# A decoder layer on one core: 512 KB transfers cut into quarters, other buffers for the end's temporaries, new dates for the planner

## The chip, the cores and the metric

The kernel runs on one core of one Trainium2 chip. The core has four engines that compute: PE (TensorE, matrix products), DVE (VectorE), ACT (ScalarE) and POOL (GpSimd). SP (SyncE) issues nearly all DMAs here. The metric is the device time of one execution in microseconds (us); lower is better.

## The reference

One decoder layer over 8 batches of 512 rows and 256 columns, in float32, each of its three parts followed by a layer norm:

```python
# gated linear attention in chunks of 32 rows, with decay
S = jnp.einsum('bncd,bnkd->bnck', Qc, Kc) * mask
O = jnp.einsum('bnck,bnkd->bncd', S, Vc).reshape(B, T, D)
x1 = ln(x + (sigmoid(x @ W_g.T) * O @ W_o.T + x))
# cross attention, 16 heads of 64, over a context of 512 rows
a = softmax(where(key_mask, q @ k.T / 8, -inf))
x2 = ln(x1 + ((a @ v) @ Wo + bo))
# FFN, 1024 wide: ternary weights, a low-rank term, squared relu
h = bitlinear(x2, w_fc) + gate * (x2 @ v.T @ fast_b.T @ u.T)
out = ln(x2 + bitlinear(relu(h)**2, w_proj))
```

## The kernel before

The kernel keeps float32 accuracy by splitting each operand into two float16 halves, high and low, and adding three products of halves (`PASSES`, line 43). A split is two instructions: one engine casts the high half, another subtracts it from the source.

**Units.** The bulk is the cross attention. `units` holds one entry for each batch b, pair of heads p (8 of them) and quarter of 128 query rows qt (4): 256 units. Line 451 issues all instructions, so the profile is read by tile names. For one unit, `scores` computes `s` for two heads on PE, DVE adds the mask and takes the extreme (`s`, `nm`), ACT takes the exponential (`e`). `split_p` casts `e` into the high half of `ph`, on ACT or on POOL as `HIGH` says (a or p for qt 0 to 3; the first word is for batch 0, the second for the later ones, the third for pairs 5 to 7 of the last batch), and DVE subtracts for the low half. Two units share one DMA transpose of `ph` into `pT` (1 MB of float16, issued by SP), and `attend` multiplies it with `v` into `av`. After four units `of` and `oh` scale and split the result, and a DMA transpose makes `oT` of it. The last two pairs of the last batch go through smaller pieces, `ofl` and `ohl`, and through PE instead of a DMA.

**Other work between the units.** Generators hold it: `gen_l0` (linear attention of the next batch; it loads `xs` and `row`), `load_ctx` (loads `ctxs` and the mask), `gen_kv`, `gen_q` and `gen_v` (projections), `gen_wo` and `gen_ffn` (output projection and FFN of the batch before), and in batch 0 the preparation of the weights. A `Filler` takes a share of them at each unit; `PULL` is the budget for one unit. `ffn_end` normalizes a finished batch and stores it. The FFN of the last batch has its own form, `ffn_tail`, in two halves of 256 rows, whose steps write `rhl`.

**The planner.** No order is written out by hand. Every instruction is recorded with a date (`nc.prio`): the unit's number plus an offset of `LATE` for its kind of work. `Recorder.cost` gives it a duration, and `Recorder.schedule` plays the engines through: whenever an engine is free it gets the ready instruction with the earliest date whose tiles have a free buffer. `REACH` bounds how far past the first candidate it looks. The order found so is emitted, one queue for each engine. SP's queue holds loads, stores and transposes in one line. The dates are thus numbers that change the order on all engines and not the instructions.

**The end.** After the last unit the fixed numbers `TP` date the rest: `bf.drain` (what remains of batch 6's FFN), the last `attend`s, `wo_tail`, the two halves of `ffn_tail`, and batch 6's `ffn_end`.

**Buffers.** A tag is a ring of buffers that a tile waits for. The change touches `t4` (5), `tmp2` (4), `pT` (3), `ph` (3), `x1T` (2) and `ctxh` (2).

Of the kernel before, what the change touches and what calls it, by code (L numbers as in the profile page):

```python
# [11 lines left out]
F16 = mybir.dt.float16  # L12
# [14 lines left out]
LAG = 4  # L27
BURST = 2
MARGIN = 0.0
REACH = 9.52  # L30
SPARE = 1
DLATE = 1.6
PTS = 3
PHS = 3
NWP = 4
TP = (0.35, 0.96, 1.15, 3.0, 0.5, 5.1)
STICK = 2.09
HOLD = 0.18
HIGH = ("apaa", "paaa", "papp")
LATE = {"k": 0.0, "q": 0.0, "v": 0.53, "w": -0.33, "l": -0.41, "o": -0.91, "f": 0.31, "s": 0.0, "a": 0.91, "t": 0.0, "x": 0.31, "e": 0.0, "c": -1.28, "d": -0.95}  # L40
PULL = {"k": 5.13, "l": 2.62, "w": 3.61, "f": 4.71, "g": 5.48}

PASSES = ((0, 0), (0, 1), (1, 0))

# [109 lines left out]
class Recorder:  # L154
# [96 lines left out]
    def cost(self, o, ins, outs):  # L251

        n = max([int(np.prod(x.shape[1:])) for x in outs + ins] or [0]) if o.engine != "PE" else outs[0].idx.size
        psum = any(x.t.pool[:2] == "ps" for x in ins + outs)
        ones = sum(x.idx.size == 1 and x.t.free > 0 for x in ins)
        o.half, o.port = None, o.engine == "POOL"
        o.dma = o.method[:3] == "dma"
        if o.dma:
            x = (outs or ins)[0]
            if o.method == "dma_start_transpose":  # L260
                blocks = n / 128
                o.occ, o.lat = 0.1 * blocks + 0.4, 0.115 * blocks + 0.55
            else:
                size = {F32: 4, F16: 2}.get(x.t.dt, 1)
                o.occ, o.lat = 0.45, n * size * x.shape[0] / (380e3 if self.prio < 0 else 210e3) + (1.2 if size == 1 else 0.1)
        elif o.engine == "PE":
            o.occ = n / 2400 + 0.0025
            o.lat = o.occ + 0.17
            if ins[0].p1 - ins[0].p0 == 64:
                o.half = ins[0].p0  # L270
        elif o.engine == "DVE":
            lat = 0.145 + n * 1.042e-3
            if o.method == "tensor_tensor_reduce":
                o.occ, o.lat = 0.615, 0.8
                return
            if not psum and o.method in ("tensor_copy", "tensor_scalar") and n >= 512:
                lat = 0.12 + n * 0.62e-3
            if psum and ones and o.method == "scalar_tensor_tensor":
                lat += 0.065
            if n <= 8:  # L280
                lat = 0.19 if o.method == "reciprocal" else 0.175 if o.method == "bn_aggr" else 0.145
            o.occ, o.lat = lat - 0.085, lat
            o.port = not psum and o.method in ("tensor_tensor", "scalar_tensor_tensor", "tensor_scalar", "tensor_copy")
        elif o.engine == "ACT":
            lat = 0.165 + n * 0.83e-3 + (0.0 if psum else 0.04) + 0.07 * ones
            o.occ, o.lat = (lat + 0.01, lat + 0.12) if "accum_out" in o.kw else (lat - 0.11, lat)
        elif o.engine == "POOL":
            if o.method == "tensor_tensor":
                lat = 0.3 + n * 1.67e-3 if n <= 512 else 0.2 + n * 1.9e-3
                if o.args[3] == ALU.pow:  # L290
                    lat = 0.42 + 0.16 * n
            else:
                lat = 0.13 + n * 0.9e-3 if n > 512 else 0.92 if n == 256 and o.kw == {} and o.method == "tensor_scalar" and o.args[-1] == ALU.is_lt else 0.62 if n > 256 else 0.56 if n > 8 else 0.22 + n * 5e-3
            o.occ, o.lat = lat - 0.03, lat
# [178 lines left out]
def decoder_kernel(ctx: ExitStack, tc: tile.TileContext, ins: dict, out: bass.AP):  # L473
# [270 lines left out]
    def split_in(src, b, nm, ring):  # L744
        stg = wk.tile([128, 2, 2, T], F32, tag="pT", name=f"{nm}s{b}", bufs=PTS)[:, 0] if ring and b == 1 else t4(f"{nm}s{b}", [128, 2, T], F32)
        sv = src[:, b * T:(b + 1) * T].rearrange("(c p) n -> p c n", p=128)
        if ring and b != 1:
            xh = t4(f"{nm}h{b}", [128, 2, 2, T])
        else:
            xh = wk.tile([128, 2, 2, T], F16, tag="ctxh", name=f"{nm}h{b}", bufs=2)  # L750
        if b == 0:
            for c in range(2):
                nc.sync.dma_start(stg[:, c], sv[:, c])
        else:
            nc.sync.dma_start(stg, sv)

        def cast():
            if b == 0:
                for c in range(2):
                    nc.scalar.copy(xh[:, 0, c], stg[:, c])  # L760
                    nc.vector.tensor_tensor(xh[:, 1, c], stg[:, c], xh[:, 0, c], ALU.subtract)
            else:
                for c in range(2):
                    nc.gpsimd.tensor_scalar(xh[:, 0, c], stg[:, c], 1.0, 1.0, ALU.mult, ALU.mult)
                    nc.gpsimd.tensor_tensor(xh[:, 1, c], stg[:, c], xh[:, 0, c], ALU.subtract)
        return xh, cast
# [60 lines left out]
    def gen_l0(b):  # L827
# [32 lines left out]
            nc.vector.tensor_tensor(v0[:, 1, 2 * tt:2 * tt + 2, :], pv, v0[:, 0, 2 * tt:2 * tt + 2, :], ALU.subtract)  # L860
            yield 6
        if b:
            nc.sync.dma_start(row, ins["x"][b].rearrange("(t p) n -> p t n", p=128))
        th = t4(f"th{b}", [128, 2, T], F32)
        for m in range(2):
            ps = misc(f"pg{b}{m}")
# [158 lines left out]

    def ffn_end(b):
        layernorm(b, rows[b], EPS, "c")
        nc.sync.dma_start(out[b].rearrange("(t p) n -> p t n", p=128), rows[b])

    def ffn_tail(b, i, base, step_):  # L1030
        row = rows[b]
        rh, py = {}, {}
        ts = slice(256 * i, 256 * i + 256)
        PL = 3
        for s_ in range(8 + PL):
            nc.prio = base + step_ * s_
            if s_ == 0:
                zst = ffn_z(b, ts, f"{b}_{i}", ("zst", "sph")[i])
            if s_ < 8:
                j = s_  # L1040
                r4 = ffn_h(b, j, ts, zst, f"{b}_{i}", True)
                hl = t4(f"rhl{i}{j}", [128, 2, 256])
                if i == 0 or j % 2:
                    nc.scalar.activation(r4, r4, AF.Square)
                else:
                    nc.vector.tensor_tensor(r4, r4, r4, ALU.mult)
                if j % 2:
                    nc.scalar.copy(hl[:, 0], r4)
                else:
                    nc.vector.tensor_copy(hl[:, 0], r4)  # L1050
                (nc.vector if j % 3 == 2 or (i == 1 and j == 7) else nc.gpsimd).tensor_tensor(hl[:, 1], r4, hl[:, 0], ALU.subtract)
                rh[j] = hl
            if s_ >= PL:
                j = s_ - PL
                if j == 0:
                    for t in range(2):
                        py[t] = misc(f"pyl{i}{t}")[:, :D]
                hl = rh.pop(j)
                for t in range(2):
                    for a in range(2):  # L1060
                        nc.tensor.matmul(py[t], hl[:, a, t * 128:(t + 1) * 128], tpj[:, j, :],
                                         start=(j == 0 and a == 0), stop=(j == 7 and a == 1))
            yield
        for t in range(2):
            tt = 2 * i + t
            y = tmp2(f"yl{tt}", [128, D])
            nc.vector.tensor_tensor(y, py[t], s2b, ALU.mult)
            nc.vector.tensor_tensor(row[:, tt], row[:, tt], y, ALU.add)
            layernorm(b, row, EPS, "c", tt, 1, True)
            nc.sync.dma_start(out[b, tt * 128:(tt + 1) * 128], row[:, tt, :])  # L1070
        yield
# [61 lines left out]
    def attend(u):  # L1133
# [12 lines left out]
        if tail:  # L1146
            if qt == 0:
                oT[b, p] = wk.tile([128, 2, T], F16, tag="oT", name=f"oT{b}_{p}", bufs=8)
            if qt % 2:
                d = den[b, p][:, qt - 1:qt + 1, :]  # L1150
                nc.vector.reciprocal(d, d)
                of = tmp2(f"ofl{p}{qt}", [128, 2, 2, DH])
                nc.vector.scalar_tensor_tensor(of, av[b, p][:, qt - 1:qt + 1], sc, d.unsqueeze(3).broadcast_to([128, 2, 2, DH]), ALU.mult, ALU.mult)
                oh = tmp2(f"ohl{p}{qt}", [128, 2, 2, 128], F16)
                ofv = of.rearrange("p t h n -> p t (h n)")
                nc.scalar.copy(oh[:, 0], ofv)
                nc.vector.tensor_tensor(oh[:, 1], ofv, oh[:, 0], ALU.subtract)
                dst = oT[b, p][:, :, (qt - 1) * 128:(qt + 1) * 128].rearrange("p a (t n) -> p a t n", t=2)
                for a in range(2):
                    pe_T(dst[:, a], [oh[:, a, t_] for t_ in range(2)], f"o{p}{qt}{a}", a)  # L1160
            return
# [85 lines left out]
    def at(i, off):  # L1247
        now[0], nc.prio = i, i + off
# [84 lines left out]
            if pend:  # L1333
                attend(pend.pop(0))

    at(U, 1)
    bf.drain()
    at(U, TP[0])
    rest(len(pend) - 4)
# [63 lines left out]
```

## Time and profile before

| | us |
|---|---|
| median of 3 runs | 1062.81 |
| these runs, lowest and highest | 1061.47, 1063.2 |
| the profiled execution, device time | 1061.94 |
| its span | 1060.1 |
| PE, DVE, ACT and POOL busy in it | 998.2, 986.9, 879.4, 544.8 |
| mean granted clock of PE | 0.988 |

The span runs from the first instruction of the profile to the last; the device time lies 1.84 us above it. A row of busy time by stretches has the stretch, its length, the busy time of each engine with its number of instructions, PE's granted clock, the DMA engines' share and GB/s. In a timeline a row is start, length, engine, operation, tile written and tiles read, and in brackets how long the engine was idle before and what released it. The rows of transfers have KB and the median time from issue to landing. PE's matmuls are pipelined and their ends are modelled, so that a PE at 20.00 of 20 need not be at its peak.

### The profile page before, as it was taken

The page shows a single profiled execution, that of the slowest core. Times are in us where ns is not written, and L with a number is a line of the kernel's source. Part 1 is how long each engine was busy: PE and PEld are TensorE (multiplying, and loading weights), DVE is VectorE, ACT ScalarE, POOL GpSimd, SP SyncE. Part 2 cuts the span into 40 slices and gives each one's busy share as a digit, 9 for nine tenths or more (in the row PEclk, how much of TensorE's full clock was granted, in tenths as well). Part 3 has the DMA queues.
Part 4 walks back from the last instruction along what each step waited for, and adds up shares of the span by engine and source line. Part 5 has one row for each costly group of instructions (what it writes and reads, how often), then busy time and mean ns, then how long its engine had stood idle before and what let it go on. Part 6 is the DMA issues. An engine that isn't in the chain of part 4 may idle for free.

```text
span 1060.1 us, 29949 instructions
## 1 busy us (share of the span) xinstructions
PE 998.2 (94%) x11976; PEld 639.3 (60%) x11976; DVE 986.9 (93%) x2101; ACT 879.4 (83%) x1876; POOL 544.8 (51%) x513
## 2 busy tenths in 40 slices
PE   7986889999999999999999999999999999999986
PEld 4644545665666656665666656766567656665664
DVE  7999989999999989999899989999899998998976
ACT  7787778889977998789977898879977889878836
POOL 0251282256841596245861577426962548443635
PEclk9999989999999999999999999999999999999989
DMA  8289799999999999989999999999999999999861
GB/s 306 99 147 186 133 214 186 164 180 191 186 185 189 174 179 168 207 155 189 185 184 204 162 185 179 192 189 156 195 163 214 154 185 170 187 167 201 138 115 41
DMA packets 646636, 185.65 MB, mean 175 GB/s; under 512 B 628448, under 2 KB 641376, under 8 KB 646496
## 3 DMA queue, kind: packets, MB, share of 16 engines
q1 hardware_dynamic: 645632, 183.42, 95.6%
q8 instruction: 93, 1.52, 0.6%
q10 hardware_dynamic: 864, 0.32, 0.1%
q14 instruction: 47, 0.39, 0.1%
HBM read 21.18 MB, written 4.19 MB: 24 GB/s over the span
## 4 chain that ended last, share of the span: by engine, by line
PE 41%; ACT 17%; DVE 17%; DMA 12%; issue 6%; POOL 4%; SPq 2%; ACTq 0%; POOLq 0%; DVEq 0%
PE av L451 8%; PE s L451 8%; DMA pT<-ph 6%; ACT e L451 6%; DVE s L451 5%; DVE ph L451 5%; PE pk L451 4%; PE pq L451 4%; PE pwo L451 4%; ACT r L451 4%; PE py L451 3%; PE pvv L451 3%; ACT ph L451 3%; SPq L451 2%; DVE W L451 2%
## 5 line engine op out<-in xcount | busy, mean ns | idle before, releaser
L451 ACT ACTIVATE e<-s,nm 128x512 f32<-128x512 f32 x512 | 354.4, 705 | 100.7 <-DVE nm L451 83.3
L451 DVE SCALAR_TENSOR_TENSOR ph<-e,ph 128x1024 f16<-128x1024 f32 x256 | 330.6, 1298 | 27.6 <-ACT ph L451 25.2
L451 DVE CUSTOM_DVE_ANT_0 s<-s,mb 128x512 f32<-128x512 f32 x512 | 342.3, 710 | 6.1 <-PE s L451 4.5
L451 PEld LDWEIGHTS <-pT 128*128 128x128 f16 x6144 | 198.7, 99 | 59.5 <-issue 29.5
L451 PE MATMUL av<-v,pT 128*128 128x64 f16 x6144 | 213.2, 194 | 12.4 <-DMA pT<-ph 12.2
L451 PE MATMUL s<-W 64*128 64x512 f16 x1536 | 205.6, 379 | 12.5 <-ACT e L451 10.8
L451 ACT ACTIVATE ph<-e 128x1024 f16<-128x1024 f32 x186 | 200.0, 1081 | 2.4 <-DMA pT<-ph 0.3
L451 POOL TENSOR_SCALAR ph<-e 128x1024 f16<-128x1024 f32 x70 | 84.8, 1211 | 227.3 <-ACT e L451 214.7
L451 PEld LDWEIGHTS <-W 64*128 64x128 f16 x1536 | 64.2, 94 | 110.4 <-issue 59.4
L451 PEld LDWEIGHTS <-wqkv 128*128 128x128 f16 x768 | 70.3, 98 | 82.6 <-issue 18.0
L451 POOL TENSOR_TENSOR oh<-of,oh 128x512 f16<-128x512 f32 x62 | 86.6, 1396 | 65.0 <-ACT oh L451 63.1
L451 ACT ACTIVATION_READ_ACCUMULATOR e<-s,nm 128x1 f32 x512 | 113.5, 222 | 0.0
L451 PE MATMUL pk<-ctxh,wqkv 128*128 128x512 f16 x384 | 103.0, 382 | 6.2 <-POOL ctxh L451 6.1
L451 PE MATMUL pvv<-wqkv,ctxh 128*128 128x256 f16 x768 | 102.0, 274 | 0.3 <-DVE v L451 0.3
L451 POOL TENSOR_TENSOR rh<-r,rh 128x512 f16<-128x512 f32 x56 | 75.1, 1345 | 52.4 <-ACT rh L451 52.4
L451 PE MATMUL pq<-x1T,wqkv 128*128 128x512 f16 x384 | 97.2, 380 | 0.5 <-DVE bob L451 0.3
L451 PEld LDWEIGHTS <-ctxh 128*128 128x128 f16 x768 | 71.4, 98 | 26.1 <-issue 13.0
L451 PEld LDWEIGHTS <-oT 128*128 128x128 f16 x768 | 73.8, 100 | 20.8 <-issue 5.3
L451 PE MATMUL pwo<-wo,oT 128*128 128x256 f16 x672 | 84.2, 276 | 0.4 <-ACT e L451 0.4
L451 DVE DVE_READ_ACCUMULATOR2_ANT nm<- 128x1 f32 x512 | 72.4, 141 | 0.0
L451 PE MATMUL ph<-x2T,tfc 128*128 128x512 f16 (+1 forms) x288 | 68.4, 356 | 0.3 <-ACT r L451 0.3
L451 PE MATMUL py<-tpj,rh 128*128 128x256 f16 x448 | 58.4, 273 | 0.0
(190 smaller groups left out, 1492.4 us busy)
## 6 DMA issues: line engine op xcount, KB each, us to landing
row<-in_x SPq DMA_DIRECT2D x8, 512.0 KB, 5.4
xs<-in_xT SPq DMA_DIRECT2D x7, 512.0 KB, 4.9
ctxs<-in_ctxT SPq DMA_DIRECT2D x7, 512.0 KB, 4.5
out_dram<-row SPq DMA_DIRECT2D x7, 512.0 KB, 3.6
wqs<-in_wqkv SPq DMA_DIRECT2D x6, 512.0 KB, 7.2
pT<-ph SPq DMA_TRANSPOSE x131, 7.5
wos<-in_wo SPq DMA_DIRECT2D x4, 256.0 KB, 2.8
fcs<-in_w_fc SPq DMA_DIRECT2D x2, 512.0 KB, 4.9
```

The source lines that it names most:

```text
L451: getattr(real[x.engine], x.method)(*[r(a) for a in x.args], **{k: r(a) for k, a in x.kw.items()})
```

## The change

First, transfers: the loads of `xs` and `ctxs` (for batches 1 to 7), those of `row` (batches 1 to 7) and the stores of batches 0 to 6, each 512 KB in one DMA, are issued as four DMAs of 128 KB. Second, buffers at the end: the eight `rhl` tiles of each half of `ffn_tail` become one tile each, in a `pT` and a `ph` buffer; `yl` and `ofl` move from `tmp2` to `x1T`, `ohl` from `tmp2` to `ctxh`. Third, dates: `REACH`, `TP` (which gets a seventh number, for `bf.drain`), `HIGH`, `LATE`, `PULL`, and the planner's duration of a float32 matmul.

```diff
-REACH = 9.52
+REACH = 9.84
...
-TP = (0.35, 0.96, 1.15, 3.0, 0.5, 5.1)
+TP = (0.0, 2.0, 0.8, 3.0, 0.5, 5.1, 2.0)
...
-HIGH = ("apaa", "paaa", "papp")
-LATE = {"k": 0.0, "q": 0.0, "v": 0.53, "w": -0.33, "l": -0.41, "o": -0.91, "f": 0.31, "s": 0.0, "a": 0.91, "t": 0.0, "x": 0.31, "e": 0.0, "c": -1.28, "d": -0.95}
-PULL = {"k": 5.13, "l": 2.62, "w": 3.61, "f": 4.71, "g": 5.48}
+HIGH = ("aapp", "paaa", "appa")
+LATE = {"k": 0.0, "q": 0.0, "v": 0.53, "w": -0.48, "l": -0.41, "o": -0.91, "f": 1.36, "s": 0.0, "a": 0.91, "t": 0.0, "x": 0.31, "e": 0.0, "c": -1.28, "d": -1.57}
+PULL = {"k": 4.04, "l": 2.62, "w": 3.61, "f": 4.71, "g": 4.5}
...
-            o.occ = n / 2400 + 0.0025
+            o.occ = n / 2400 + 0.0025 if ins[0].t.dt is F16 else n / 200
...
-            nc.sync.dma_start(stg, sv)
+            for c in range(2):
+                for h in range(2):
+                    nc.sync.dma_start(stg[:, c, 256 * h:256 * h + 256], sv[:, c, 256 * h:256 * h + 256])
...
-            nc.sync.dma_start(row, ins["x"][b].rearrange("(t p) n -> p t n", p=128))
+            for t in range(4):
+                nc.sync.dma_start(row[:, t], ins["x"][b, t * 128:(t + 1) * 128])
...
-        nc.sync.dma_start(out[b].rearrange("(t p) n -> p t n", p=128), rows[b])
+        for t in range(4):
+            nc.sync.dma_start(out[b, t * 128:(t + 1) * 128], rows[b][:, t])
...
+        rhl = wk.tile([128, 8, 2, 256], F16, tag=("pT", "ph")[i], name=f"rhl{i}", bufs=(PTS, PHS)[i])
...
-                hl = t4(f"rhl{i}{j}", [128, 2, 256])
+                hl = rhl[:, j]
...
-            y = tmp2(f"yl{tt}", [128, D])
+            y = wk.tile([128, D], F32, tag="x1T", name=f"yl{tt}", bufs=2)
...
-                of = tmp2(f"ofl{p}{qt}", [128, 2, 2, DH])
+                of = wk.tile([128, 2, 2, DH], F32, tag="x1T", name=f"ofl{p}{qt}", bufs=2)
...
-                oh = tmp2(f"ohl{p}{qt}", [128, 2, 2, 128], F16)
+                oh = wk.tile([128, 2, 2, 128], F16, tag="ctxh", name=f"ohl{p}{qt}", bufs=2)
...
-    at(U, 1)
+    at(U, TP[6])
     bf.drain()
```

## The prediction

> **What bounds the kernel now.** I read the busy line of the page first, then the chain of work that ended last, then busy time by stretches of 20 us, and last the waits of each engine inside the stretches that have gaps.
>
> ```profile
> PE 998.2 (94%) x11976; PEld 639.3 (60%) x11976; DVE 986.9 (93%) x2101; ACT 879.4 (83%) x1876; POOL 544.8 (51%) x513
> ```
> ```profile
> PE 41%; ACT 17%; DVE 17%; DMA 12%; issue 6%; POOL 4%; SPq 2%; ACTq 0%; POOLq 0%; DVEq 0%
> ```
>
> PE and DVE are busy together, and no engine carries the chain alone. So a time saved on one engine counts only where the other has a gap at the same place. The stretches (PE, PEld, DVE, ACT, POOL busy, clock, DMA) show where that is:
>
> ```profile
> 80.00:100.00 20.00, 14.18 (x184) 8.28 (x181) 19.22 (x50) 17.06 (x37) 4.69 (x5) 1.00 0.94 168
> 240.00:260.00 20.00, 19.58 (x197) 10.56 (x194) 19.88 (x45) 19.88 (x41) 12.23 (x14) 1.00 1.01 192
> 260.00:280.00 20.00, 19.42 (x223) 11.82 (x222) 15.92 (x29) 19.53 (x41) 19.10 (x17) 1.00 1.02 182
> 280.00:300.00 20.00, 20.00 (x260) 13.41 (x257) 20.00 (x48) 16.00 (x35) 13.06 (x13) 1.00 1.04 177
> ...
> 1020.00:1040.00 20.00, 18.00 (x204) 13.94 (x203) 13.93 (x46) 11.74 (x30) 7.41 (x15) 0.91 0.12 23
> 1040.00:1060.00 20.00, 10.97 (x88) 7.54 (x86) 11.99 (x34) 11.50 (x28) 10.93 (x19) 0.88 0.16 53
> ```
>
> Added up over all such rows (20 less PE's busy time), PE idles 21.8 us in 40 to 160 (batch 0, where the weights are still prepared), 16.2 us in all of 160 to 960, and 16.4 us from 960 on. The middle repeats every 122 to 124 us, and its one weak place per batch is the row 260 to 280: ACT full, DVE at 15.9. The timeline of DVE there says why:
>
> ```profile
> 267.13 1.32 DVE L451 SCALAR_TENSOR_TENSOR ph<-e,ph 128x1024 f16<-128x1024 f32 x1 [3.60 <-ACT ph L451]
> ```
>
> DVE waits 3.60 us for ACT's half of a split (`ph`), because ACT is working off `r`, its square and its cast for the FFN of the batch before. The same wait (3.54 to 3.60) comes back at 389, 513, 635, 757 and 881.
>
> **The change part by part.**
>
> *Quarters.* 7 loads of `xs`, 7 of `ctxs`, 7 of `row` (batch 0's stays) and 7 stores become 112 transfers, 84 issues more.
>
> ```profile
> out_dram<-row SPq DMA_DIRECT2D x7, 512.0 KB, 3.6
> ...
> out_dram<-row SPq DMA_DIRECT2D x4, 128.0 KB, 1.7
> ```
> ```profile
> 305.43 0.52 SPq L451 DMA_DIRECT2D out_dram<-row  x1
> 306.36 5.64 SPq L451 DMA_TRANSPOSE pT<-ph  x1
> ```
>
> An issue holds SP's queue for 0.52 us, so 84 cost it 44 us. The queue's transposes hold it 131 x 4.94 + 62 x 1.3 + 14 x 3 = 770 us of 1060, so there is room on the average; but a `pT` transpose issued right behind a group comes 3 x 0.52 = 1.6 us later than now. Queued behind are only transposes, and PE's `av` waits for those:
>
> ```profile
> PE av L451 <- DMA pT<-ph: 12.2, 10, 2.4
> ```
>
> The gain is bounded by those of the 10 waits that stand beside a transfer that is cut: 1.64 us at 139.75 (loads at 136.3 and 136.9) and 1.21 at 921.5 (a store at 918.1), 2.9 together; the others, 2.42 and 2.28 at 963 and 1015 above all, have only transposes before them. The loss, if every delay were bare, is 28 x 1.6 = 45 us. Both ends are far from the usual case: 10 waits on 131 `pT` transposes mean that nearly every one of them has slack, so I stay near nothing: -0.5.
>
> [...] The two rows above (3.6 and 1.7) agree that a quarter costs far more than a quarter, but nobody waits for these loads in the middle, and no run yet shows four of them issued behind one another.
>
> *Dates of the middle* (`LATE["f"]` 0.31 to 1.36, `PULL["k"]` 5.13 to 4.04, `LATE["d"]`, `REACH`). No instruction is added or removed. The FFN's work of the batch before loses priority against split and softmax by a whole unit, which is the wait of 3.60 us above; what is late next is PE, idle in the six ACT-bound rows by 0.58 + 0.78 + 1.07 + 1.21 + 1.61 + 1.21 = 6.5 us. If the six DVE waits (21.5 us) went altogether, PE's 16.2 us of gaps would be the limit. Below nothing: the FFN's pieces put off must be done before their batch ends, in rows where DVE or PE stands at 20.00, and the 9.7 us of PE gaps outside the six rows are as good a size for a loss as for a gain. Nearest to the row of the six gaps, less than half of it: -2.5.
>
> *Batch 0* (`HIGH[0]` from apaa to aapp, `LATE["w"]`, the planner's cost of an f32 matmul). Eight splits go from ACT (1.065 us each, 8.5 in all) to POOL (1.047, 8.4). PE waits 7.0 us for ACT's `e` between 60 and 160, the bound of the gain. The price is on DVE, which is at 20.00 from 20 to 80 and at 19.22 in the next row: its `ph` takes 1.19 us alone and 2.02 beside POOL work:
>
> ```profile
> 999.86 1.19 DVE L451 SCALAR_TENSOR_TENSOR ph<-e,ph 128x1024 f16<-128x1024 f32 x1
> ...
> 1004.73 2.02 DVE L451 SCALAR_TENSOR_TENSOR ph<-e,ph 128x1024 f16<-128x1024 f32 x1
> ```
>
> So 0 to 8 x 0.83 = 6.6 us more, and POOL's 29.2 us of waiting for ACT's `e` there say that it has the time itself. Two f32 matmuls (`ps`, 1.21 us, after a wait of 2.15 for `dg`) are now known to the planner as long, worth about 1 us. Halves of both bounds cancel (-3.5 and +3.3); I take -1 with that one.
>
> [...]
>
> *The end* (`HIGH[2]` from papp to appa, `TP`, buffers, `PULL["g"]`). From 983 to 1008 the chain is DVE. Three more splits leave POOL: 3 x 0.83 = 2.5 us at most off DVE, while ACT idles 2.01 and 2.52 us before its `e` at 1001.8 and 1007.6 and so can take 1.065 each; I take -1.5. The drain of batch 6 put off by one unit takes `y` (0.67, in the chain at 1004.13) out of the way: -0.5. From 1032 to 1052 ACT is the limit (17.06 of 20 busy). The waits for `rhl` there (1.12, 0.42, 0.49 on ACT) are for the ring of three that holds `r4`, which stays; no wait names the ring of five that `rhl` leaves. So the new buffers free the order rather than remove a wait: between 0 and 2.9 us (20 less 17.06); with the earlier start of the first half's steps (0.8 apart for 1.15) I take -1. Below nothing: three splits that delay ACT's `e` by 1.065 each, +3.2. Together -3, between -6 and +3.
>
> **Sum.** -0.5 - 2.5 - 1 - 3 = -7.0 against the profiled execution: span 1060.1, device time 1061.94, so 1054.9. The median of the three runs, 1062.81, lies 0.87 above that execution; added, 1055.8.
>
> **Rivals.**
> (1) *SP's queue becomes the wait.* Quarters are issued in a row ahead of transposes that have no slack. PE's weight loads for `av` already wait in 23 places and PE in 10, so a third of the 28 groups is thinkable: 28 x 1.6 / 3 = 15 us, less the 6.5 of the other parts, 1062.8 + 8.5 = 1071. It decides from where 6.5 of the 45 us is bare, that is from one group in seven (4 of 28). For it: DMA shares of 1.0 to 1.2 in the middle. Against: 290 us free in the queue.
> (2) *The new dates only move the gaps.* PE and DVE are at 20.00 in the rows after 280, and the work that fills the gap is missed there; only a microsecond or two of the end remains: 1061.5.
> (3) *The ACT-bound row dissolves.* All of PE's 16.2 us in the middle go, and the end gives 3: 1062.8 - 19.2 = 1043.6. For it: ACT has 4 us free in the row behind. Against: in 280 to 300 DVE and PE are both full already.
>
> **How the numbers follow.** The forecast gets 0.54, rival 1 0.20, rival 2 0.14, rival 3 0.12. Less than 0.2% (2.1 us) can't be told from no change, so faster is 0.54 + 0.12 = 0.66, same 0.14, slower 0.20. The forecast's own range is 1055.8 with -7 and +5: half of the bounds of the middle and the end. The asked range reaches to rival 1 at 1071 and, below, to 1046, which leaves out half of rival 3 and the larger half of rival 1's bad cases.
>
> **What would show it.** Quarters: PE's wait for `pT` stays near 12 us, and SP shows groups of four issues or ones parted by transposes; a wait above 20 means rival 1. Middle: the six DVE waits of 3.6 us are gone or shorter, the period of a batch falls by about 0.4 us from 122 to 124; if the period stands, rival 2. Batch 0: POOL's `ph` count is 75 for 70, DVE's mean `ph` there rises from 1.29 us. End: from the last `e` to the last store less than the 50 us of now, DVE's `ph` near 1004 at 1.2. The prediction is wrong if the period grows, or if DVE's extra time in batch 0 is paid in full.

## The result, and the profile after

| | before | after |
|---|---|---|
| median (lowest to highest, runs), us | 1062.92 (1061.47 to 1063.2, 4) | 1076.02 (1072.72 to 1078.71, 4) |
| ratio, 95% interval | | 1.0125 (1.0109 to 1.0141) |
| profiled execution, span, us | 1061.94, 1060.1 | 1075.25, 1073.5 |
| mean granted clock of PE | 0.988 | 0.980 |

The changed kernel is 1.25% slower, 13.1 us by the medians; 1055.8 had been forecast, within 1046 to 1071. The page after, its busy line and its chain of work that ended last:

```profile
PE 1002.4 (93%) x11976; PEld 639.3 (60%) x11976; DVE 995.0 (93%) x2101; ACT 879.6 (82%) x1871; POOL 552.8 (51%) x518
...
PE 42%; DVE 26%; DMA 10%; ACT 9%; issue 7%; POOL 6%; SPq 0%; ACTq 0%; DVEq 0%; POOLq 0%
```

PE runs the same 11,976 matmuls in 4.2 us more, DVE the same 2101 instructions in 8.1 us more. ACT's part of the chain fell from 17% to 9% and DVE's rose from 17% to 26%: ACT, which the forecast saw as the weak place of the middle, holds less of the chain, and the time is longer.

**Where the time went.** DVE adds the mask to each unit's scores (`s`), so the start of that instruction dates a unit. Differences of these dates (units 0 to 31 are batch 0, 224 to 255 the last batch) give the stages, in us; each row adds up to its span:

| from, to | before | after | difference |
|---|---|---|---|
| start, unit 0 | 45.4 | 45.1 | -0.3 |
| 0, 16 | 57.3 | 69.6 | +12.3 |
| 16, 32 | 65.4 | 63.7 | -1.7 |
| 32, 224 | 730.2 | 742.1 | +11.9 |
| 224, 255 | 109.7 | 105.3 | -4.4 |
| 255, last instruction | 52.1 | 47.6 | -4.5 |

So batch 0 lost 10.6, the six middle batches 11.9, and the end won 8.9. The stretches of after (PE, PEld, DVE, ACT, POOL busy, granted clock, DMA share, GB/s):

```profile
80.00:100.00 20.00, 13.27 (x172) 7.82 (x168) 15.78 (x39) 11.64 (x26) 6.97 (x7) 0.74 0.95 173
...
270.30:290.30 20.00, 16.58 (x179) 8.71 (x176) 17.01 (x28) 19.51 (x41) 19.87 (x16) 1.00 1.14 192
290.30:310.30 20.00, 19.87 (x259) 13.75 (x256) 20.00 (x43) 15.84 (x33) 13.53 (x12) 1.00 1.09 189
```

Batch 0: from 80 to 100 DVE went from 19.22 busy to 15.78 and the clock from 1.00 to 0.74. Middle: unit 32 comes 10.3 us later in after, so its rows are set 10.3 us later than those of before from 260 on. There DVE rose only from 15.92 to 17.01, while PE fell from 19.42 to 16.58 and ACT stayed full (19.53 and 19.51); the next rows are nearly alike. The ends are compared by their distance from the last instruction, since after's comes 13.4 us later. The two stretches from 60 to 20 us ahead of it, of before and then of after:

```profile
1000.10:1020.10 20.00, 17.03 (x267) 13.47 (x263) 16.86 (x33) 8.13 (x22) 9.56 (x7) 0.91 1.18 189
1020.10:1040.10 20.00, 18.00 (x204) 14.02 (x203) 13.93 (x46) 11.84 (x30) 7.51 (x15) 0.91 0.11 22
```
```profile
1013.50:1033.50 20.00, 19.01 (x289) 13.88 (x288) 18.55 (x38) 17.06 (x38) 10.36 (x8) 1.00 1.21 199
1033.50:1053.50 20.00, 19.64 (x241) 16.23 (x240) 15.96 (x47) 11.59 (x30) 10.81 (x18) 1.00 0.22 51
```

PE idles 5.0 us of these 40 before and 1.4 after, and DVE 9.2 and 5.5: the end is denser.

**Batch 0.** PE's timeline of after (start, length, what, and in brackets the idle time before it), then the same place of before:

```profile
79.51 1.57 PE L451 MATMUL av<-v,pT 128*128 128x64 f16 x48
86.03 2.74 PE L451 MATMUL av<-v,pT 128*128 128x64 f16 x48 [4.95 <-DMA pT<-ph]
88.71 1.88 PE L451 MATMUL s<-W 64*128 64x512 f16 x7
```
```profile
78.07 0.82 PE L451 MATMUL s<-W 64*128 64x512 f16 x6
...
80.51 0.82 PE L451 MATMUL s<-W 64*128 64x512 f16 x6
83.12 1.57 PE L451 MATMUL av<-v,pT 128*128 128x64 f16 x48 [1.80 <-DMA pT<-ph]
```

In before, scores of later units go ahead of the `av` that waits for a transpose; the wait is 1.80 us, and DVE has scores to work on. In after, the next scores (unit 10's) stand behind that `av`: PE is idle for 4.95 us, DVE starts no scores between 74 and 90.3, and both pieces then run at a granted clock of 0.51 (the mean from 84.9 to 95.1), the `av` in 2.74 us for 1.57. The order of SP's queue changed as well. Its timeline, of before and then of after:

```profile
73.51 2.53 SPq L451 DMA_TRANSPOSE tfc<-fct  x2
76.21 4.89 SPq L451 DMA_TRANSPOSE pT<-ph  x1
```
```profile
70.01 2.50 SPq L451 DMA_TRANSPOSE tfc<-fct  x2
72.61 9.82 SPq L451 DMA_TRANSPOSE pT<-ph  x2
```

In before the third `pT` goes ahead of two transposes of the FFN's weights (`tfc`), in after behind them, and it waits for the low half of the sixth `ph`, which ends at 71.1 for 67.8, since DVE did other work first. The fourth `pT`, for which the `av` at 86.03 waits, then follows with no gap: it starts 1.3 us later than in before, and the `av` behind it 2.9 us later.

### The profile page after: what moved, and what is told of

It reads as the page before. It is cut to its first block, busy times and chain, and to the rows that moved or that the text cites. A ratio compares the mean times of both kernels' runs of the same rounds, so it can differ in the third digit from the quotient of the medians.

```text
span 1073.5 us, 30062 instructions
## 1 busy us (share of the span) xinstructions
PE 1002.4 (93%) x11976; PEld 639.3 (60%) x11976; DVE 995.0 (93%) x2101; ACT 879.6 (82%) x1871; POOL 552.8 (51%) x518
## 4 chain that ended last, share of the span: by engine, by line
PE 42%; DVE 26%; DMA 10%; ACT 9%; issue 7%; POOL 6%; SPq 0%; ACTq 0%; DVEq 0%; POOLq 0%
PE s L451 8%; DVE s L451 8%; PE av L451 8%; DMA pT<-ph 8%; DVE ph L451 7%; PE pwo L451 5%; PE pvv L451 4%; ACT e L451 4%; PE pq L451 3%; PE pk L451 3%; DVE W L451 2%; PE py L451 2%; POOL ctxh L451 2%; PE pv L451 1%; ACT r L451 1%
## 5 line engine op out<-in xcount | busy, mean ns | idle before, releaser
L451 ACT ACTIVATE e<-s,nm 128x512 f32<-128x512 f32 x512 | 349.9, 692 | 94.5 <-DVE nm L451 79.9
L451 DVE SCALAR_TENSOR_TENSOR ph<-e,ph 128x1024 f16<-128x1024 f32 x256 | 338.2, 1333 | 19.8 <-ACT ph L451 15.8
L451 PEld LDWEIGHTS <-pT 128*128 128x128 f16 x6144 | 201.5, 99 | 69.8 <-issue 35.1
L451 PE MATMUL av<-v,pT 128*128 128x64 f16 x6144 | 216.4, 194 | 18.7 <-DMA pT<-ph 15.1
L451 PE MATMUL s<-W 64*128 64x512 f16 x1536 | 209.2, 386 | 7.1 <-ACT e L451 5.9
L451 ACT ACTIVATE ph<-e 128x1024 f16<-128x1024 f32 x181 | 192.4, 1067 | 2.0 <-ACT e L451 0.4
L451 POOL TENSOR_TENSOR oh<-of,oh 128x512 f16<-128x512 f32 x62 | 91.6, 1478 | 100.9 <-ACT oh L451 83.2
L451 ACT ACTIVATION_READ_ACCUMULATOR e<-s,nm 128x1 f32 x512 | 106.1, 207 | 0.0
L451 PE MATMUL pvv<-wqkv,ctxh 128*128 128x256 f16 x768 | 94.1, 273 | 0.6 <-ACT e L451 0.6
L451 POOL TENSOR_TENSOR rh<-r,rh 128x512 f16<-128x512 f32 x56 | 77.8, 1397 | 25.5 <-ACT rh L451 24.9
```

The costliest lines, as they stand in the source:

```text
L451: getattr(real[x.engine], x.method)(*[r(a) for a in x.args], **{k: r(a) for k, a in x.kw.items()})
```

## The experiments

Theory P: nearly all of the time comes from the order that the planner finds anew. Its input is all costs and dates at once; any edit of one of them gives another order on all engines, and the old order was a good one. The first expectations call it theory O, there with the addition that the quarters themselves cost nothing. Theory Q, the rival of the prediction: the quarters themselves hold up SP's queue. Theory R: single dates, those of batch 0 above all, do the harm by what they move. All times are compared with the kernel before on the same chip, whose medians there were 1061.6 to 1063.0. `Recorder.schedule` adds up the length of its own plan; that sum of assumed costs is no measurement, but is given beside some results, since it tells whether a loss was in the plan already (before 1032.9 us, after 1039.0).

### The transfers alone, with the order kept

**quarters_in_place.** Before's order on every engine, instruction for instruction; the planner sees one transfer with the whole's cost, and where it stood, four are emitted in a row.

```diff
+            nc.joint = []
             for t in range(4):
                 nc.sync.dma_start(row[:, t], ins["x"][b, t * 128:(t + 1) * 128])
+            nc.joint[0].lat = (nc.joint[0].lat - 0.1) * 4 + 0.1
+            nc.joint = None
...
```

> The order of before on every engine, unchanged; only each of the 28 transfers of 512 KB is issued as four of 128 KB, in a row, where the one stood. Theory O (the new order costs the 13 us, the quarters themselves nothing): within 0.3% of before, 1060 to 1066 us. Theory Q (the quarters hold up SP's queue and the transposes behind them): 1068 to 1076 us, and PE's wait for pT above 15 us.

Measured: 1068.66 us (1064.58 to 1072.74, 6 runs), ratio 1.005 (1.0023 to 1.0076). SP's timeline of this kernel, and PE's wait for `pT`:

```profile
305.86 2.02 SPq L451 DMA_DIRECT2D out_dram<-row  x4
308.29 5.51 SPq L451 DMA_TRANSPOSE pT<-ph  x1
```
```profile
PE av L451 <- DMA pT<-ph: 14.9, 12, 2.3
```

The store takes SP 2.02 us for 0.52, so the transpose behind starts at 308.29 for 306.36. Over the whole run only two more of PE's waits for `pT` come of it (12 for 10) and 2.7 us. But the profile puts the whole loss into units 32 to 224 (738.3 us for 730.2), and there the wait, in before and then here, is

```profile
PE av L451 <- DMA pT<-ph: 1.4, 2, 0.9
```
```profile
PE av L451 <- DMA pT<-ph: 5.7, 5, 1.7
```

These 4.3 us are most of the 5.4 that PE idles longer in this stage (19.4 for 14.0); the rest of the 8.1 is PE's busy time (718.9 for 716.2). Quarters are a loss of 5 us (2.4 to 8.1) in this order: the mechanism of rival 1 at a third of its price. The time lies in the range of theory Q, though the wait stays just under its 15 us; that quarters cost nothing here was wrong.

**whole_in_place.** The counterpart: after's order kept, each group of four emitted as one transfer of 512 KB (a load at the place of its first quarter, a store at that of its last).

```diff
+        at = {id(o): n for n, o in enumerate(self.ops)}
+        for g, n, args in self.groups:
+            g.sort(key=lambda o: at[id(o)])
+            for o in g:
+                o.parts = [] if o is not g[n] else None
+            g[n].args, g[n].kw = args, {}
...
```

> The changed kernel's order on every engine, unchanged; only each group of four transfers is issued as one of 512 KB (a load where its first quarter stood, a store where its last stood). If the transfers cost the same here as the other way round (quarters in the old order: 0.5% slower), this is 4 to 8 us faster than the changed kernel, 1068 to 1072 us, and 1.0% or less above before. If the quarters help in the order that was planned for them, it is slower than the changed kernel, 1077 us or more.

Measured: 1075.49 (1075.08 to 1079.78, 5 runs), ratio 1.0142 (1.0116 to 1.0168); after has 1.0125 (1.0109 to 1.0141). Its wait for `pT`, and that of after:

```profile
PE av L458 <- DMA pT<-ph: 11.5, 12, 4.9
```
```profile
PE av L451 <- DMA pT<-ph: 15.1, 15, 5.0
```

Without the quarters the wait is 3.6 us shorter and the time the same. I had thought that quarters cost in any order; in the new one they cost nothing that can be measured. By the far ends of the two intervals the cuts could account for 2.7 of the 13 us at most. Theory Q falls for this result: most of the 13 us comes with the new order, with whole transfers as with cut ones.

### Planned anew: sizes changed, dates left

**quarters_old_dates.** Before with all transfers cut and nothing else, planned anew.

```diff
-            nc.sync.dma_start(row, ins["x"][b].rearrange("(t p) n -> p t n", p=128))
+            for t in range(4):
+                nc.sync.dma_start(row[:, t], ins["x"][b, t * 128:(t + 1) * 128])
...
-        nc.sync.dma_start(out[b].rearrange("(t p) n -> p t n", p=128), rows[b])
+        for t in range(4):
+            nc.sync.dma_start(out[b, t * 128:(t + 1) * 128], rows[b][:, t])
...
```

> Before with all quarters, planned anew, and nothing else changed (old dates, old buffers). Theory P: the old dates fit the old sizes, so this is the slowest of all, 1078 to 1095 us, and the changed kernel's dates have won a part of it back. Theory Q: as the quarters in the old order, 1065 to 1072 us. If the new dates themselves are the harm: about 1066 to 1070 us.

Measured: 1082.01 (1079.81 to 1083.79, 4 runs), ratio 1.0192 (1.0173 to 1.021). The same cut costs 5 us where the order is kept and 20 where the planner makes a new one (plan 1048.9). After, with its dates, `HIGH` and buffers, is 6 us faster than this. In the profiles the gain lies at the end: from unit 224 on this kernel takes 158.5 us and after 152.9, while batch 0 (129.4 and 133.3) and the middle (744.2 and 742.1) show no gain in sum. So the new dates of batch 0 and of the middle did not mend what the cut cost.

**row1_quartered.** Before with one transfer of 28 cut: the load of `row` for batch 1.

```diff
+            if b == 1:
+                for t in range(4):
+                    nc.sync.dma_start(row[:, t], ins["x"][b, t * 128:(t + 1) * 128])
...
```

> Before with one load alone in quarters: row of batch 1, at the very start; planned anew with the old dates. Theory P (what costs is the order that the planner finds once a transfer's size changes, not the transfer): in the new order SP's transpose of the FFN weights (tfc) stands before the third pT instead of behind it, the first 16 units take 65 to 70 us instead of 57, PE's granted clock falls to half after a wait for pT there, and the whole takes 1070 to 1080 us. Theory Q (each quartered transfer costs a little on SP's queue): one load of 28, 1062 to 1065 us.

Measured: 1081.81 (1075.59 to 1084.91, 4 runs), ratio 1.0184 (1.0149 to 1.0218). Three issues more, 1.6 us of SP's queue, and 20 us of time. Units 0 to 16 take 70.6 us (69.6 in after), SP takes `tfc` ahead of the third `pT` as in after, and PE's timeline shows after's wait:

```profile
82.09 1.08 PE L451 MATMUL s<-W 64*128 64x512 f16 x6
87.09 1.51 PE L451 MATMUL av<-v,pT 128*128 128x64 f16 x25 [3.92 <-DMA pT<-ph]
```

No date and no `HIGH` differs from before here. So a loss of this size in batch 0 needs neither `HIGH[0]` nor more than one cut load; the order is enough.

**whole_replanned.** After with whole transfers, planned anew: the dates without the sizes that they were given with.

```diff
-            for t in range(4):
-                nc.sync.dma_start(row[:, t], ins["x"][b, t * 128:(t + 1) * 128])
+            nc.sync.dma_start(row, ins["x"][b].rearrange("(t p) n -> p t n", p=128))
...
```

> The changed kernel with its transfers whole again (512 KB each), planned anew. Theory O: still slower than before by 0.5% or more, 1068 to 1080 us, since dates and HIGH stay. Theory Q: back to 1055 to 1064 us.

Measured: 1083.15 (1077.52 to 1087.2, 4 runs), ratio 1.0187 (1.0136 to 1.0238). That is slower than either theory allowed. Old dates with new sizes and new dates with old sizes lose 1.9% each, new dates with new sizes 1.25%: none of the three orders made anew is as good as the old one, and a set of dates does not carry its worth to other sizes.

### One date or word at a time

**batch0_high.** Before with the word of batch 0 alone.

```diff
-HIGH = ("apaa", "paaa", "papp")
+HIGH = ("aapp", "paaa", "papp")
```

> Before with HIGH of batch 0 alone moved (apaa to aapp: eight more splits on POOL). The prediction's term: within 1061 to 1065 us, bounds -7 and +6.6. Theory P: beyond its upper bound, 1072 to 1085 us, the first 16 units in 65 us or more, because the order of the weights' preparation changes with it, not because of 6.6 us on DVE.

Measured: 1080.23 (1079.48 to 1080.69, 4 runs), ratio 1.0163 (1.0133 to 1.0194). Units 0 to 16 take 69.2. Taken alone this would put the loss on the word; the next run speaks against it.

**start_back.** After with batch 0's word and `LATE["w"]` as in before.

```diff
-HIGH = ("aapp", "paaa", "appa")
+HIGH = ("apaa", "paaa", "appa")
-LATE = {... "w": -0.48, ...}
+LATE = {... "w": -0.33, ...}
```

> The changed kernel with batch 0's HIGH (apaa) and the weights' date LATE w (-0.33) as before. Theory O, in the form that these two cause the 12.3 us by which the first 16 units are late: 1062 to 1067 us, the first 16 units again in 57 to 60 us. Theory Q: 1072 to 1078 us.

Measured: 1086.58 (1084.62 to 1088.76, 4 runs), ratio 1.0223 (1.0191 to 1.0256): another 10 us slower than after, outside both ranges, with 71.5 for units 0 to 16. My theory R falls: the new word costs when it comes alone, and taking it back, together with `LATE["w"]`, costs too.

**ffn_later.** Before with the FFN's date alone, the main part of the step on which I had put -2.5.

```diff
-LATE = {... "f": 0.31, ...}
+LATE = {... "f": 1.36, ...}
```

> Before with LATE f alone moved (0.31 to 1.36), the main term of the prediction for the middle (-2.5 us there, -6.5 at best). If that term holds by itself: 1055 to 1061 us, and DVE's six waits of 3.6 us are gone. Theory P (any shift from before's dates loses the fit): the waits of 3.6 us go and the time still rises, 1066 to 1076 us, PE idle for longer in batches 1 to 6.

Measured: 1076.65 (1075.26 to 1077.81, 4 runs), ratio 1.013 (1.0103 to 1.0157). Batch 0 is that of before here (57.3 and 65.2), so the middle is seen by itself: 747.3 for 730.2. Two of its waits:

```profile
DVE ph L451 <- ACT ph L451: 17.4, 23, 1.5
...
PE pk L451 <- POOL ctxh L451: 12.6, 14, 1.6
```

DVE's long wait is gone (longest 1.5 for 3.6), as predicted; PE waits for other things in its place (for `ctxh` 6.1 us in before).

**date_shift.** Before with one date moved by a twentieth of a unit. A theory of local effects expects next to nothing.

```diff
-LATE = {... "q": 0.0, ...}
+LATE = {... "q": 0.05, ...}
```

> Before with one date moved by a twentieth of a unit (LATE q 0.0 to 0.05), nothing else. Theory P: even that gives another order in batches 1 to 6 and costs there, 1067 to 1078 us, with batch 0 and the end as before. Theory Q and any theory of a certain part of the change: 1061 to 1065 us.

Measured: 1085.64 (1084.53 to 1086.43, 4 runs), ratio 1.0223 (1.0206 to 1.024). In every batch of the middle the second 16 units take 68 to 70 us for 62.5 to 64. PE's two longest waits there in the first of them, and the clock behind them; the next batches have the same pair at 389 and 392, 516 and 520, 644 and 647:

```profile
262.10 1.02 PE L451 MATMUL ph<-x2T,tfc 128*128 128x512 f16 x4 [1.75 <-DVE of L451]
...
265.55 0.47 PE L451 MATMUL pk<-ctxh,wqkv 128*128 128x512 f16 x1 [2.19 <-DVE v L451]
```
```profile
265.70:269.10 3.40, 3.40 (x42) 2.20 (x40) 2.19 (x3) 3.40 (x11) 3.40 (x3) 0.50 1.16 218
```

This is the clearest run for theory P: no engine gets other work, only another order, and the smallest of the edits has one of the two largest effects. Batch 0 is that of before, as theory P said; the time lies above its range.

### The end

**end_alone.** Before with `HIGH[2]`, the seven numbers of `TP`, the new buffers and `PULL["g"]` 4.5.

```diff
-TP = (0.35, 0.96, 1.15, 3.0, 0.5, 5.1)
+TP = (0.0, 2.0, 0.8, 3.0, 0.5, 5.1, 2.0)
...
-HIGH = ("apaa", "paaa", "papp")
+HIGH = ("apaa", "paaa", "appa")
...
```

> Before with the end's part of the change alone: HIGH of the last pairs (appa), TP, the other buffers, PULL g. The changed kernel's last batch and end are 8.8 us shorter than before's; both theories expect that most of it comes from this part: 1052 to 1058 us. If it needs the new middle as well, 1060 to 1064.

Measured: 1058.2 (1055.32 to 1062.48, 10 runs), ratio 0.9957 (0.994 to 0.9975). **end_no_buffers** is the same without the new buffers:

```diff
-        rhl = wk.tile([128, 8, 2, 256], F16, tag=("pT", "ph")[i], name=f"rhl{i}", bufs=(PTS, PHS)[i])
...
-                hl = rhl[:, j]
+                hl = t4(f"rhl{i}{j}", [128, 2, 256])
...
```

> The end's part alone (HIGH of the last pairs, TP, PULL g) on before, with the old buffers for rhl, yl, ofl and ohl. If the dates and HIGH bring the end's gain: 1057 to 1060 us, as with the buffers (1058). If the buffers bring it: 1061 to 1064 us, no faster than before.

Measured: 1060.41 (1057.04 to 1063.2, 12 runs), ratio 0.9977 (0.996 to 0.9994). By the ratios the end is a gain of 4.6 us, and about half of that is there without the buffers; the two intervals overlap, so the split is not firm.

**end_shorter_plan.** end_alone with three dates chosen so that the plan is short (1028.7):

```diff
-TP = (0.0, 2.0, 0.8, 3.0, 0.5, 5.1, 2.0)
+TP = (0.0, 1.8, 0.8, 3.0, 0.5, 5.1, 2.0)
...
-LATE = {... "v": 0.53, ...}
+LATE = {... "v": 0.61, ...}
...
-PULL = {... "g": 4.5}
+PULL = {... "g": 3.84}
```

> The end's part as in end_alone (HIGH, other buffers, TP, g) with three dates moved a little further so that the planner's own plan gets 3.3 us shorter (v 0.61, TP 1.8 for 2.0, g 3.84); transfers whole, all other dates of before. Theory P says that on the chip such a plan is faster by about as much as it is shorter: 1052 to 1057 us, faster than both kernels. If the plan's length says nothing, 1056 to 1065.

Measured: 1053.64 (1053.19 to 1056.27, 6 runs), ratio 0.9919 (0.9898 to 0.9941). It is faster than both kernels, and by the ratios 4 us faster than end_alone, whose plan is 3.3 us longer (1032.0). Its busy line, and the same stretch of the last batch in before and in this kernel (the batch begins at 898.3 and 897.5):

```profile
PE 990.6 (94%) x11976; PEld 636.0 (60%) x11976; DVE 982.4 (93%) x2101; ACT 883.7 (84%) x1879; POOL 544.4 (52%) x510
```
```profile
960.00:980.00 20.00, 17.58 (x204) 10.10 (x203) 15.41 (x29) 16.37 (x35) 7.16 (x6) 0.91 1.16 195
```
```profile
960.00:980.00 20.00, 17.67 (x222) 10.53 (x218) 19.91 (x39) 19.02 (x42) 8.00 (x8) 1.00 1.12 202
```

Batch 0 and the middle are nearly before's (57.3, 65.2 and 728.8); the last batch falls from 109.7 to 102.0 us. DVE, at 15.41 here before, is at 19.91. The rest after the last unit stays at 52.0.

## Why the prediction was wrong, point by point

The step that failed lies under all four terms: each prices the change of single waits in before's order, and that the planner makes another order out of every such edit was put at nothing. The sum was -7.0 and the medians say +13.1; by stages the middle gave +11.9 for -2.5, batch 0 +10.6 for -1 and the end -8.9 for -3.

**Quarters, -0.5.** Right in where the cost would be and in that most transposes have slack: PE's wait for `pT` is 15.1 us, not above 20, and whole_in_place leaves 2.7 us at most where rival 1 had 15. By themselves quarters cost 5.3 us in the old order, ten times the term and with the other sign, and nothing measurable in the new. What I left out is that the planner sees 84 instructions more and makes its order anew. The four loads of a group do not run one after another, as the profile of after shows.

```profile
xs<-in_xT SPq DMA_DIRECT2D x28, 128.0 KB, 3.0
row<-in_x SPq DMA_DIRECT2D x28, 128.0 KB, 3.3
```

SP takes 1.82 us for the four issues of `xs` at 536.46 and 2.84 for those at 661.54, and a quarter lands 3.0 us (median) after its own issue, so that the four overlap. An issue takes 0.43 (median). An estimate from these numbers is that the fourth quarter lands 4.4 to 5.4 us after the first was issued (1.82 and 2.84, less 0.43, and 3.0), against 4.9 for one whole load of `xs` in before.

**The middle, -2.5.** Here the step failed by most. What it named came true: DVE's wait for ACT's `ph`

```profile
DVE ph L451 <- ACT ph L451: 15.8, 19, 1.5
```

fell from 25.2 us with 3.6 as the longest to 15.8 with 1.5. What followed did not: the period of a batch rose from 121.7 to 123.7 us (730.2 and 742.1 over 6), which the prediction had named as a sign of being wrong. ffn_later shows the step alone: `LATE["f"]` by itself costs 14 us. I had taken DVE's gap for the weak place, had written that what is late next is PE, and had bounded a loss by 9.7 us of PE's old gaps. Late next was ACT, as it had been. Units 24 to 27 of batch 2, in before and in after:

```profile
375.60:392.90 17.30, 16.09 (x187) 8.88 (x186) 13.55 (x26) 17.30 (x36) 15.97 (x15) 1.00 1.00 187
```
```profile
389.40:409.50 20.10, 17.60 (x196) 9.86 (x195) 16.70 (x33) 20.02 (x42) 18.82 (x16) 1.00 1.05 192
```

ACT is full in both, and in after it has 2.7 us more to do there. In the six middle batches together PE idles 7.5 us in these four units before and 17.4 after: 9.9 of the 10.8 us that it idles longer from unit 32 to 224. (The four units ahead are some 2.5 us shorter in after; the second halves of the batches hold 10.7 of the 11.9 us.)

That DVE's wait was no measure of the time is seen across orders. The groups of `ph` on DVE in date_shift and in end_shorter_plan (busy, mean ns, idle time before it):

```profile
L451 DVE SCALAR_TENSOR_TENSOR ph<-e,ph 128x1024 f16<-128x1024 f32 x256 | 337.1, 1325 | 7.0 <-ACT ph L451 4.8
```
```profile
L451 DVE SCALAR_TENSOR_TENSOR ph<-e,ph 128x1024 f16<-128x1024 f32 x256 | 325.2, 1279 | 28.6 <-ACT ph L451 26.5
```

The order with the smallest wait, 4.8 us, is the second slowest of all; the one with the whole wait, 26.5, is the fastest. Before has 25.2. The wait was harmless, since PE had work at that time (19.42 of 20 in the row from 260). The stretch from 160 to 960 as one row, for before, after, date_shift and end_shorter_plan, shows what went with the time:

```profile
160.00:960.00 800.00, 783.84 (x9661) 501.67 (x9658) 763.63 (x1597) 690.51 (x1454) 437.38 (x393) 1.00 1.03 181
```
```profile
160.00:960.00 800.00, 774.75 (x9489) 494.81 (x9489) 756.90 (x1560) 680.25 (x1424) 440.31 (x395) 1.00 1.04 180
```
```profile
160.00:960.00 800.00, 767.53 (x9379) 493.63 (x9380) 749.79 (x1543) 673.63 (x1407) 433.55 (x382) 0.99 1.00 176
```
```profile
160.00:960.00 800.00, 783.46 (x9681) 502.15 (x9678) 761.47 (x1604) 692.26 (x1455) 437.29 (x391) 1.00 1.04 182
```

PE idles 16.2, 25.3, 32.5 and 16.5 us of the same 800. DVE 36.4, 43.1, 50.2 and 38.5. In the two slower orders both do less in the same time, and PE's idle time is made of many short waits (`ctxh`, `pT`, `e`, `of`). As all four kernels give PE the same matmuls, its idle time is the loss seen from PE's side and not a cause of its own. The new gaps could not be bounded from the old order's gaps.

**Batch 0, -1.** This step failed too, by more than its bounds (-7 to +6.6): +10.6. The named price came in small: POOL does its 8 more `ph` there (75 for 70 in all), and DVE's mean `ph` rose from 1284 to 1339 ns, 0.06 x 32 = 1.8 us, far below the 6.6 of the prediction. Not named was that DVE would wait for POOL's half: 3.0 us in after, nothing in before. (POOL's own mean in batch 0 is 1.24 us in before and 1.21 in after, not 1.05.) The rest goes with the order: scores behind a waiting `av`. A loss of this size in units 0 to 16 (57.3 in before, 69.6 in after) also comes from cutting one load (70.6), from the word alone (69.2) and without the word (71.5).

**The end, -3.** Right in sign, and too small: -8.9 in after's stages, outside its bounds of -6 to +3, and -4.6 by the ratio of end_alone, within them. Which of its terms was undersized is not shown; that of buffers and earlier steps, -1, is the likeliest, since PE's idle time from 60 to 20 us ahead of the last instruction alone fell by 3.6 us (5.0 to 1.4) and DVE's by 3.7. Of two `ph` of DVE near the end, one runs at 1.2 as I had said, with POOL idle, and one is still beside POOL, whose `rh` runs from 1016.94 for 1.16 us:

```profile
1017.38 1.80 DVE L451 SCALAR_TENSOR_TENSOR ph<-e,ph 128x1024 f16<-128x1024 f32 x1
...
1023.47 1.19 DVE L451 SCALAR_TENSOR_TENSOR ph<-e,ph 128x1024 f16<-128x1024 f32 x1
```

**The rivals.** None of the three was it. Each, and the forecast too, moves single waits in an order taken as given. The case that was missing is that the order itself changes everywhere, at a price not tied to the size of the edit: five edits of before that were planned anew (all quarters, one load, one word, two single dates) gave +14 to +24 us. Gains appear only where the edit is to the end: end_alone, end_no_buffers and end_shorter_plan, the last with dates chosen for a short plan. The plan's length parts the orders made by the planner into two groups: the four of 1028.7 to 1033.0 us, before among them, are the fastest on the chip (1053.6 to 1062.9), and the eight of 1038.9 to 1048.9 all lose (1076.0 to 1086.6). Within the second group it says little: date_shift's 1040.1 gives 1085.6, and quarters_old_dates' 1048.9 gives 1082.0. The chip loses more than the plan says: after is 6.1 us longer in its plan and 13.1 on the chip.

**Open.** How much of batch 0's 10.6 us is waiting and how much is the half clock that follows it; which of the many moved instructions in the middle costs what; and what `HIGH[0]` would cost with before's order kept, since it was run only in orders made anew.

## What to carry to other kernels

Where a planner makes the order, an edit is two edits: the new instruction, and a new order on all engines. Price the first by putting the new form into the old order, and expect the second to lose by some 1 to 2% until the dates are chosen again. The planner's own sum, to be had without a run, was 6.1 us longer for after; it had the right sign where the sum of single waits had the wrong one. The longest wait of a full engine is not yet a weak place: ask first which engine is full at that place, here ACT, and whether it stays so after the change.

## What the runs showed of the hardware

In units 0 to 31 of after PE's granted clock is 0.50 in five stretches, of 10.2, 10.2, 6.8, 3.4 and 3.4 us, and 1.00 between them. The first lies around the wait at 86 us (PE's busy time is the first number behind the length, the clock stands behind POOL):

```profile
81.50:84.90 3.40, 0.00 (x0) 0.00 (x0) 2.71 (x8) 2.12 (x4) 2.22 (x3) 1.00 1.38 178
84.90:95.10 10.20, 7.72 (x76) 4.34 (x77) 7.05 (x16) 4.73 (x11) 2.20 (x2) 0.51 0.87 165
95.10:98.50 3.40, 3.40 (x58) 2.10 (x56) 3.40 (x9) 3.29 (x9) 1.05 (x1) 0.97 1.04 241
```

PE's last matmul ahead of the wait ends at 81.1; the clock falls near 85.0, 3.9 us later, and is back near 95.2. Ahead of the third stretch, from 126 on, PE did not stand still throughout:

```profile
126.00:129.40 3.40, 1.74 (x14) 0.79 (x12) 3.40 (x8) 2.03 (x6) 0.20 (x1) 1.00 0.29 55
129.40:136.20 6.80, 6.80 (x63) 3.70 (x62) 4.38 (x11) 4.26 (x11) 1.05 (x1) 0.50 0.80 140
```

Here 1.74 us of work in 3.40 is followed by 6.8 us at 0.50, in which PE is busy throughout. After a wait of 1.80 us, before's at 83.12, the clock stays at 1.00 (the mean from 80 to 100). Why it fell at these places and not at others is not shown.

Over units 0 to 31, after has 34 us at a clock of 0.50 (10.2 + 10.2 + 6.8 + 3.4 + 3.4), before 10.2 (three times 3.4). An estimate from these: lost time is at most half of that, 17 against 5, so the clock could account for up to 12 us, as much as batch 0 lost. Two other runs show that the two do not go together in step. Over these units whole_replanned has a mean clock of 0.95, date_shift one of 0.92 (before 0.96, after 0.87); the first takes 4.7 us longer than before, the second 0.4.
